# Two graph layers on one core: where the loads of x, of the turned x1 and of the transposed codes are issued

## The chip, the cores and the metric

The kernel runs on one core of a Trainium2 chip. Its engines are TensorE (PE, with its weight loads listed apart as PEld), VectorE (DVE), ScalarE (ACT), GpSimd (POOL) and SyncE (SP). SP, ACT and POOL also issue DMA transfers, each from its own instruction stream and in that stream's order. The metric is device time in microseconds, the median of several runs of the whole kernel; lower is better.

## The reference

Two layers work on x (4096 x 512, float32) with one 0/1 matrix adj (4096 x 4096, about 0.8% ones). In the code below, cut to what matters, `ln` is a normalisation of each row.

```python
# layer 0: mean over the first 64 neighbours
Ab   = adj > 0
keep = Ab & (cumsum(Ab, axis=1) <= 64)
cnt  = keep.sum(axis=1, keepdims=True)
xj   = leaky_relu((keep @ x) / maximum(cnt, 1) @ W_nb.T + b_nb)
xi   = leaky_relu(x @ W_line.T + b_line)
x1   = ln(x + xi + where(cnt > 0, xj, 0))

# layer 1: attention over the neighbours
Wh  = x1 @ W + bW
e   = leaky(Wh @ a1 + b1)[:, None] + (Wh @ a2 + b2)[None, :]   # slope 0.2 on the sum
att = softmax(where(adj > 0, e, -9e15), axis=1)
out = ln(x1 + att @ Wh)
```

## The kernel before

The 4096 rows are cut into 32 blocks of 128. The order of the instructions on each engine is the order in which the program writes them, and waits on data and on buffers are added to it. A pool of n buffers makes the n+1st tile wait until the first is no longer read or written. There are four stages.

**Maps of layer 0 (loop over i at L332 to L375, 0 to 272 us).** For each block i, PE turns x (`turn_x`, four 128x128 transposes into `pt`, copied to `xt` by ACT), one block ahead, and multiplies the turned block by the two weight matrices (`linear`, L288, eight matmul instructions each). ACT copies the first product to `y_hi`, DVE keeps the remainder in `y_lo` (L373). DVE's `own(i)` (L319 to L321) adds bias, activation and x to the second product and stores it to `own_d`; its last operation (L321) is the last reader of the tile `xb` of x, which has four buffers. So `load_x(i + 2)` (L238, a DMA issued by ACT for i of 3 and above) needs `own(i - 2)` to be done. From block 5 on the loop also makes codes of adj (`codes_until`): SP loads a piece of 2048 columns (`a`, 1 MB), ACT makes `edge` of it, DVE scans it (`left`, L169, and the product at L174), ACT packs the result to bytes (`code`, L192) and POOL stores it to `code_d`. 22 of the 64 pieces are made in this stage. Before the codes, in block 2, DVE folds the layer-1 weights (`fold_w`) and SP stores the 4 KB result in 4-byte elements (`wa_d`) and loads it back spread over the partitions (`wa_row`).

**Sums of layer 0 (272 to 736 us).** PE adds up, for each block, 64 products of 0/1 maps (`kt`, made by ACT from transposed codes) with `y_hi` and `y_lo` (L433). The remaining codes are made beside it, and finished blocks go through the normalisation and are stored to `x1_d`.

**Maps of layer 1 (loop over i at L656, 736 to 869 us).** For each block, `wh` = x1 times W (L661, eight matmul instructions). x1 comes back from `x1_d` already arranged (`load_turned(i + 3)`, L469: four DMAs of 64 KB issued by ACT), DVE finishes the turn in 32x32 squares (`turn_x1(i + 2)`, L491), PE multiplies. The tile `x1b` has four buffers, so the load of block b needs block b-4 to have been turned by DVE. Blocks 0 and 1 are loaded by SP in another form and turned on PE. In the same loop SP loads untransposed codes (`nat`, one buffer, `load_nat`, L510), and in blocks 12 to 19 ACT and DVE take maxima over them (`greatest`, L523 and L527); at block 6 SP issues the four transposing loads of codes for the first group of four blocks (`load_ct(0)`, L506). At block 22 `shifts(0)` (L544, L546) has SP store eight small numbers per row (`uv_d`) and load them back spread over the partitions (`row`), once the store has landed.

**Sums of layer 1 (869 to 1765 us).** In eight groups of four blocks, ACT and DVE make the attention weights (`produce`) and PE multiplies them with `wh` (L601). In each group SP loads the transposed codes of the next one (`load_ct(g + 1)`, two buffers), nat, uv_d and row again.

The built program gives every DMA issued by SP or ACT one of eight completion semaphores in turn, so such a DMA also waits for the one that used its semaphore before, eight DMAs earlier in the program.

Of the kernel before, what the change touches and what calls it, by code (L numbers as in the profile page):

```python
# [11 lines left out]
BF16 = mybir.dt.bfloat16  # L12
# [8 lines left out]
P = 128  # L21
# [10 lines left out]
def two_layer_adj_gnn(  # L32
# [16 lines left out]
    nc = tc.nc  # L49
# [3 lines left out]
    NT = NB // 2  # L53
    CH = 2048
    NCH = N // CH
    GB = 4
# [53 lines left out]
    code_d = [dram.tile([P, N // 2], BF16, name=f"code_d{b}") for b in range(NB)]  # L110

    def transpose_to(dst, src_of, n):

        pt = ps_s.tile([P, n, P], F32, name="pt")
        for k in range(n):
            nc.tensor.transpose(pt[:, k, :], src_of(k), ident)  # L116
        nc.scalar.copy(dst, pt)  # L117
# [20 lines left out]
    with ExitStack() as l0:  # L138
# [88 lines left out]
        with ExitStack() as la:  # L227
# [7 lines left out]
            def load_x(i):  # L235
                if i < NB:
                    xbs[i] = work.tile([P, C], F32, name="xb", bufs=4)
                    (nc.sync if i < 3 else nc.scalar).dma_start(xbs[i], x_blk(i))  # L238

            def turn_x(i):  # L240
                if i < NB:
                    xts[i] = work.tile([P, NC, P], F32, name="xt")
                    transpose_to(xts[i], lambda k: xbs[i][:, ts(k, P)], NC)
# [30 lines left out]
            def turn_w(name, idle=0):  # L274

                wt = wp.tile([P, NC, C], F32, name=f"wt_{name}")
                for c in range(NC):
                    if idle:
                        spin(idle)
                    transpose_to(  # L280
                        wt[:, :, ts(c, P)], lambda k: raw[name][c][:, ts(k, P)], NC
                    )
                w_t[name] = wt

            def linear(lhs_t, name):
                pl = ps_acc.tile([P, C], F32, name="acc")
                for k in range(NC):
                    nc.tensor.matmul(  # L288
                        pl, lhs_t[:, k, :], w_t[name][:, k, :],
                        start=(k == 0), stop=(k == NC - 1),  # L290
                    )
                return pl
# [24 lines left out]
            def own(i):  # L317
                t = work.tile([P, C], F32, name="t")
                nc.vector.tensor_tensor(t, pls.pop(i), bias_line, ALU.add)  # L319
                nc.vector.scalar_tensor_tensor(t, t, 0.01, t, ALU.mult, ALU.max)  # L320
                nc.vector.tensor_tensor(t, t, xbs.pop(i), ALU.add)  # L321
                nc.gpsimd.dma_start(own_d[i], t)
# [9 lines left out]
            for i in range(NB):  # L332
                if i == 0:
                    nc.sync.dma_start(bias_line, b_line.partition_broadcast(P))
                if i > 0:
                    turn_x(i + 1)
                xt = xts.pop(i)
                pys[i] = linear(xt, "nb")
                if i == 0:
                    turn_w("line")  # L340
                pls[i] = linear(xt, "line")
                if i == 0:
                    turn_x(1)
                nc.scalar.copy(y_hi[:, i, :], pys[i])
                if i > 0:
                    own(i - 1)
                if i > 0:
                    load_x(i + 2)
                if i == 0:
                    load_w("w", w, (nc.sync,))  # L350
                if i == 1:
                    load_rows()
                    nc.gpsimd.dma_start(bias_nb, b_nb.partition_broadcast(P))
                if i == 2:
                    fold_w()
                if i == 3:
                    spread_wa()
                if i > 3:
                    codes_until(int((i - 3) * 22 / (NB - 6)) if i < NB - 3 else 22)
                if i == NB - 3:  # L360

                    spare = adj_p.tile([P, CH], I32, name="a")
                    ktbs[0] = spare[:, : CH // 2].bitcast(BF16).rearrange(
                        "p (t i) -> p t i", t=NT
                    )
                    nc.sync.dma_start_transpose(ktbs[0], code_d[0])
                if i == NB - 1:
                    spare = adj_p.tile([P, CH], BF16, name="edge")
                    kts[0] = spare.bitcast(F32R).rearrange(
                        "p (t r i) -> p t r i", r=2, i=P  # L370
                    )
                    make_kt(0)
                nc.vector.tensor_tensor(  # L373
                    y_lo[:, i, :], pys.pop(i), y_hi[:, i, :].bitcast(F32), ALU.subtract
                )  # L375
# [44 lines left out]
        for s in range(NB * NS):  # L420
            i, g = divmod(s, NS)
# [27 lines left out]
    ctp = tile_p("l1_ct", 2)  # L449
# [16 lines left out]
    x1rs, x1bs, x1ts, pws, cts, nats, uvs, ms = {}, {}, {}, {}, {}, {}, {}, {}  # L466
    p_ts, accs1, zs, zaccs, ys = {}, {}, {}, {}, {}

    def load_turned(i):  # L469

        if i < NB:
            x1rs[i] = xp.tile([P, P // SQ, NC, SQ], F32, name="x1b", bufs=4)
            for n in range(NC):
                nc.scalar.dma_start(
                    x1rs[i][ts(n, SQ)].rearrange("a j m b -> a j (m b)"),
                    x1_d[i][:, ts(n, P)].rearrange("(j a) c -> a j c", a=SQ),
                )
# [21 lines left out]
        else:  # L499
            nc.vector.tensor_tensor(wh_sum, wh_sum, wh[:, i, :], ALU.add)  # L500

    def load_ct(g):
        if g < NG:
            cts[g] = ctp.tile([P, NT, GB, P], BF16, name="ct")
            for k in range(GB):
                nc.sync.dma_start_transpose(cts[g][:, :, k, :], code_d[g * GB + k])  # L506

    def load_nat(b):
        nats[b] = xp.tile([P, N // 2], BF16, name="nat", bufs=1)
# [146 lines left out]
    for i in range(NB):  # L656
        load_turned(i + 3)
        pw = ps_acc.tile([P, C], F32, name="acc")
        x1t = x1ts.pop(i)
        for k in range(NC):  # L660
            nc.tensor.matmul(  # L661
                pw, x1t[:, k, :], ws[:, k, :], start=(k == 0), stop=(k == NC - 1)
            )
        pws[i] = pw
        turn_x1(i + 2)
        if i == 4:
            load_nat(0)
        if i == 6:
            load_ct(0)
        if 12 <= i < 12 + 2 * GB:  # L670
            greatest(*divmod(i - 12, 2))
        if i == 22:
            shifts(0)
        if i > 0:
            finish_wh(i - 1)
        if i >= NB - LEAD:
            produce(i - NB + LEAD)
# [3 lines left out]
    for q in range(LEAD, NQ + LEAD):  # L681
        g, t = divmod(q, NT)
        if q < NQ:
            produce(q)
        consume(q - LEAD)
        if q == 8:
            all_sum = ps_acc.tile([P, C], F32, name="acc")
            nc.tensor.matmul(all_sum, ones, wh_sum, start=True, stop=True)
            nc.scalar.copy(wh_sum, all_sum)
        if t == LEAD and g < NG:  # L690
            load_ct(g + 1)
            if g + 1 < NG:
                load_nat((g + 1) * GB)
        if q == NQ - 2:
            for k in range(GB):
                load_x1(NB - GB + k)
        if q == NQ + LEAD - 1:

            end_weights(NG - 1)
            for k in range(GB):  # L700
                b, base = NB - GB + k, x1bs.pop(NB - GB + k)
                share = stat.tile([P, 1], F32, name="share")
                nc.vector.tensor_tensor(
                    share, none[:, b : b + 1], zs[NG - 1][:, k : k + 1], ALU.mult
                )
                nc.vector.scalar_tensor_tensor(base, wh_sum, share, base, ALU.mult, ALU.add)
                x1bs[b] = base
            for k in range(GB):
                b = NB - GB + k
                y = ep.tile([P, C], F32, name="y", bufs=4)  # L710
                nc.vector.scalar_tensor_tensor(
                    y, accs1[NG - 1][k], zs[NG - 1][:, k : k + 1], x1bs.pop(b),
                    ALU.mult, ALU.add,
                )
                ys[b] = y, ln_stats(y)
                end_out(b, nc.sync)
            break

        if t == LEAD - 1 and g > 0:
            for k in range(GB):  # L720
                load_x1((g - 1) * GB + k)
                end_sum((g - 1) * GB + k)
            end_weights(g - 1)
        if g > 0:
            if LEAD <= t < LEAD + GB:
                end_stats((g - 1) * GB + t - LEAD)
            if LEAD < t <= LEAD + GB:
                end_out((g - 1) * GB + t - LEAD - 1, nc.gpsimd)
        if g + 1 < NG:
            if 5 <= t < 5 + 2 * GB:  # L730
                k, h = divmod(t - 5, 2)
                greatest((g + 1) * GB + k, h)
            if t == 13:
                shifts(g + 1)
# [34 lines left out]
```

## Time and profile before

| | |
|---|---|
| runs | 1764.3, 1766.97, 1770.71 us (median 1766.97) |
| profiled execution | 1767.0 us, of which the span of the trace 1764.9 us |
| PE busy | 1720.0 us (97%) |
| DVE, ACT, POOL busy | 1402.2, 875.3, 192.9 us |
| chain that ended last | PE 84%, DVE 8%, DMA 5% |
| x loads by ACT (29) | 256 KB each, median 3.2 us from issue to landing |
| turned x1 by ACT (120 DMAs) | 64 KB each, median 2.1 us to landing |
| transposing loads of codes (32) | median 5.6 us to landing |

Busy time is the sum over an engine's instructions; the span is from the first to the last of them. The chain that ended last is followed back from the end: at each step to what released the instruction, or to the one before it on its engine. The idle time of an engine matters only where that chain passes through it. A PE that is called busy in the first stage can still be waiting between short matmul groups, so that stage is read from the chain and the timelines, not from the shares.

### The profile page before, as it was taken

How to read it: one execution, taken by the hardware profiler on the slowest of the kernel's cores; microseconds unless marked ns; L12 is line 12 of the kernel's file. 1: busy time of each engine (PE TensorE's matmuls, PEld its weight loads, DVE VectorE, ACT ScalarE, POOL GpSimd, SP SyncE). 2: the span in 40 equal slices, each digit the busy share in tenths (PEclk: the TensorE clock that was granted, in tenths of full speed). 3: DMA queues.
4: the chain of work that ended last, by engine and by line, in shares of the span. 5: the costliest groups of instructions: out<-in, count | busy, mean ns of one | idle time of the engine just before them, and what ended most of it. 6: DMA issues, size and time to landing. Idle time of an engine off the chain costs nothing.

```text
span 1764.9 us, 14748 instructions
## 1 busy us (share of the span) xinstructions
PE 1720.0 (97%) x5118; PEld 949.6 (54%) x5118; DVE 1402.2 (79%) x1649; ACT 875.3 (50%) x910; POOL 192.9 (11%) x234
## 2 busy tenths in 40 slices
PE   8799999999999999989899999999999999999998
PEld 5344447888888888733344444444444444444443
DVE  3599998999999997458677986968869689696754
ACT  2355555767667674112355463644636445364331
POOL 1011112223232322100000100001000010000100
PEclk9899999999999999999999999999999999999999
DMA  4566667676767673762402304122041220411100
GB/s 143 191 220 204 205 222 204 192 221 198 221 203 210 207 204 95 133 148 79 100 25 55 88 24 96 60 64 68 24 95 56 65 68 27 96 50 46 48 0 25
DMA packets 209227, 206.57 MB, mean 117 GB/s; under 512 B 154848, under 2 KB 170240, under 8 KB 200832
## 3 DMA queue, kind: packets, MB, share of 16 engines
q1 hardware_dynamic: 174352, 145.55, 30.8%
q0 software_dynamic: 13056, 44.07, 6.6%
q10 hardware_dynamic: 21744, 16.00, 3.4%
q8 instruction: 41, 0.67, 0.2%
q14 instruction: 34, 0.28, 0.1%
HBM read 130.02 MB, written 42.00 MB: 97 GB/s over the span
## 4 chain that ended last, share of the span: by engine, by line
PE 84%; DVE 8%; DMA 5%; issue 1%; SPq 1%; ACT 1%; ACTq 0%; POOLq 0%; DVEq 0%
PE acc L601 49%; PE acc L433 26%; PE acc L288 5%; DVE left L169 3%; PE acc L661 2%; DMA xb<-in_x_dram 2%; DMA ct<-code_d 1%; SPq L506 1%; PE pt L116 1%; DMA x1b<-x_d 1%; DVE pen L527 1%; DVE t L320 1%; DVE y_lo L373 1%; DMA uv_d<-uv 1%; DVE t L319 1%
## 5 line engine op out<-in xcount | busy, mean ns | idle before, releaser
L601 PE MATMUL acc<-wh,p 128*128 128x512 f32 x2048 | 881.2, 592 | 0.0
L601 PEld LDWEIGHTS acc<-wh,p 128*128 128x128 f32 x2048 | 388.5, 190 | 486.0 <-issue 485.3
L433 PE MATMUL acc<-y_lo,kt 128*128 128x512 f32 x1016 | 395.2, 389 | 0.0
L433 PE MATMUL acc<-y_hi,kt 128*128 128x512 f32 x1016 | 395.2, 389 | 0.0
L561 ACT ACTIVATE p<-row,e 128x512 f32<-128x512 f32 x256 | 182.8, 714 | 419.1 <-PE acc L601 367.4
L564 DVE TENSOR_TENSOR p<-p,p 128x1024 f32<-128x1024 f32 x128 | 156.2, 1221 | 124.7 <-ACT p L561 124.6
L127 POOL TENSOR_TENSOR rs<-ve,neg_half 128x1 f32<-128x1 f32 x64 | 101.5, 1587 | 1152.1 <-DVE ve L125 1152.1
L221 ACT ACTIVATE kt<-ktb,steep 128x1024 fp32r<-128x1024 uint8 x124 | 142.8, 1152 | 154.2 <-PE acc L433 154.2
L433 PEld LDWEIGHTS acc<-y_hi,kt 128*128 128x128 f32 x1016 | 190.8, 188 | 39.5
L433 PEld LDWEIGHTS acc<-y_lo,kt 128*128 128x128 f32 x1016 | 190.8, 188 | 39.5
L561 ACT ACTIVATE p<-row,e_fifth 128x512 f32<-128x512 f32 x256 | 180.8, 706 | 1.4 <-DVE p L564 1.3
L566 DVE TENSOR_TENSOR p<-p,ct 128x1024 f32<-128x1024 f32 x128 | 156.8, 1225 | 4.4
L523 ACT ACTIVATE pen<-nat,far 128x2048 bf16<-128x2048 uint8 x64 | 127.3, 1990 | 63.4 <-DMA x1b<-x_d 52.1
L571 DVE TENSOR_TENSOR zacc<-zacc,p 128x1024 f32<-128x1024 f32 x120 | 147.0, 1225 | 4.1
L169 DVE TENSOR_TENSOR_SCAN left<-two,edge 128x2048 bf16<-128x2048 f32 x32 | 141.4, 4417 | 6.4 <-ACT edge L158 6.4
L169 DVE TENSOR_TENSOR_SCAN left<-two,ends,edge 128x2048 bf16<-128x2048 f32 x32 | 143.3, 4478 | 0.0
L158 ACT ACTIVATE edge<-a,steep 128x2048 bf16<-128x2048 int32 x64 | 127.5, 1993 | 17.8 <-DVE left L174 10.5
L661 PE MATMUL acc<-ws,x_t 128*128 128x512 f32 x256 | 116.0, 611 | 16.0 <-DVE x_t L491 15.8
L192 ACT CAST code<-left 128x2048 uint8<-128x2048 bf16 x64 | 120.5, 1883 | 0.8 <-DVE left L174 0.8
L288 PE MATMUL acc<-wt_nb,xt 128*128 128x512 f32 x256 | 119.2, 610 | 0.9 <-ACT wt_nb L117 0.7
L288 PE MATMUL acc<-wt_line,xt 128*128 128x512 f32 x256 | 115.2, 592 | 0.7 <-ACT wt_line L117 0.7
L661 PEld LDWEIGHTS acc<-ws,x_t 128*128 128x128 f32 x256 | 49.1, 195 | 82.4 <-issue 57.0
(103 smaller groups left out, 1029.1 us busy)
## 6 DMA issues: line engine op xcount, KB each, us to landing
a<-in_adj_dram SPq DMA_DIRECT2D x64, 1024.0 KB, 5.5
code_d<-code POOLq DMA_DIRECT2D x64, 256.0 KB, 4.4
nat<-code_d SPq DMA_DIRECT2D x32, 512.0 KB, 3.6
own_d<-t POOLq DMA_DIRECT2D x32, 256.0 KB, 4.3
own<-own_d SPq DMA_DIRECT2D x32, 256.0 KB, 2.8
x_d<-own POOLq DMA_DIRECT2D x32, 256.0 KB, 3.4
x1b<-x_d SPq DMA_DIRECT2D x32, 256.0 KB, 5.5
x1b<-x_d ACTq DMA_DIRECT2D x120, 64.0 KB, 2.1
```

The source lines that it names most:

```text
L158: nc.scalar.activation(edge_of[s], loaded.pop(s), AF.Sigmoid, bias=steep[:, 0:1], scale=STEEP)
L169: nc.vector.tensor_tensor_scan(left, two.to_broadcast([P, CH]), e, NEIGHBORS + 2.0 if h == 0 else end, ALU.max, ALU.subtract,)
L221: nc.scalar.activation(kts[s], bytes_.rearrange("p t (i r) -> p t r i", r=2), AF.Sigmoid, bias=steep[:, 1:2], scale=STEEP,)
L288: nc.tensor.matmul(pl, lhs_t[:, k, :], w_t[name][:, k, :], start=(k == 0), stop=(k == NC - 1),)
L433: nc.tensor.matmul(accs[i], kt[:, k // 2, k % 2, :], term[:, j, :], start=(j == 0 and term is y_hi), stop=(j == NB - 1 and term is y_lo),)
L523: nc.scalar.activation(pen, nats[b].bitcast(U8)[:, ts(h, HALF)], AF.Relu, bias=far, scale=-FAR)
L561: nc.scalar.activation(dst[:, r, :], uvs[g][:, k, :], AF.Exp, bias=e[:, b : b + 1])
L564: nc.vector.tensor_tensor(p0, p0, p1, ALU.max)
L566: nc.vector.tensor_tensor(p0, p0, code.rearrange("p (x r) -> p r x", r=2), ALU.min)
L571: nc.vector.tensor_tensor(zaccs[g], zaccs[g], p0, ALU.add)
L601: nc.tensor.matmul(accs1[g][k], p_[:, r, ts(k, P)], wh[:, 2 * t_ + r, :], start=(t_ == 0 and r == 0), stop=(t_ == NT - 1 and r == 1),)
L661: nc.tensor.matmul(pw, x1t[:, k, :], ws[:, k, :], start=(k == 0), stop=(k == NC - 1))
```

## The change

Three things move; no computation is added or taken away. In the maps of layer 0, `load_x(i + 2)` is issued at the top of block i, ahead of `turn_x(i + 1)`, instead of behind `own(i - 1)`; on ACT's stream it now stands before the copies of `xt` and `y_hi` of that block. In the maps of layer 1, the four DMAs of each turned x1 block are issued by SP instead of ACT, in SP's stream order with nat, uv_d, row and the transposing loads. And the four transposing loads of the first group, issued together at block 6 before, are issued one by one at blocks 8, 11, 14 and 17, each behind the x1 loads of its block; the later groups keep their four loads together.

```diff
                 if i > 0:
+                    load_x(i + 2)
                     turn_x(i + 1)
...
                 if i > 0:
                     own(i - 1)
-                if i > 0:
-                    load_x(i + 2)
...
             for n in range(NC):
-                nc.scalar.dma_start(
+                nc.sync.dma_start(
                     x1rs[i][ts(n, SQ)].rearrange("a j m b -> a j (m b)"),
...
-    def load_ct(g):
+    def load_ct(g, k):
         if g < NG:
-            cts[g] = ctp.tile([P, NT, GB, P], BF16, name="ct")
-            for k in range(GB):
-                nc.sync.dma_start_transpose(cts[g][:, :, k, :], code_d[g * GB + k])
+            if k == 0:
+                cts[g] = ctp.tile([P, NT, GB, P], BF16, name="ct")
+            nc.sync.dma_start_transpose(cts[g][:, :, k, :], code_d[g * GB + k])
...
-        if i == 6:
-            load_ct(0)
+        if i in range(8, 8 + 3 * GB, 3):
+            load_ct(0, (i - 8) // 3)
...
         if t == LEAD and g < NG:
-            load_ct(g + 1)
+            for k in range(GB):
+                load_ct(g + 1, k)
```

## The prediction

> **What bounds the kernel now.** I read the page first, then the stages, the chain of waits, and the timelines of the two stages that the change touches.
>
> Stages (start:end, sum; then PE, PEld, DVE, ACT, POOL busy, granted clock, DMA share, GB/s):
>
> ```profile
> 0.00:69.80 69.80, 58.27 (x181) 31.16 (x182) 20.85 (x48) 16.54 (x25) 6.84 (x17) 0.95 0.46 151
> 69.80:271.60 201.80, 193.01 (x513) 87.49 (x511) 197.81 (x196) 109.63 (x95) 25.17 (x47) 0.99 0.63 208
> 271.60:736.20 464.60, 464.60 (x2051) 384.60 (x2050) 407.13 (x526) 297.19 (x211) 115.54 (x107) 1.00 0.66 193
> 736.20:869.00 132.80, 116.79 (x266) 49.94 (x265) 85.18 (x129) 24.83 (x22) 2.90 (x4) 0.96 0.58 127
> ```
>
> From 271.6 to 736.2 PE never stops, and from 869.0 on it stops for 8.7 us only. Neither stage holds an edited line that can cost it anything. What can be won or lost lies before 271.6 (maps of layer 0) and in 736 to 869 (maps of layer 1); whatever moves their ends moves the kernel's end by as much, since PE-bound work follows.
>
> The chain of waits in the first stage, in order of time (start, duration):
>
> ```profile
> 33.17 3.91 DMA xb<-in_x_dram
> ...
> 41.38 9.64 DMA xb<-in_x_dram
> ...
> 57.90 3.71 DMA xb<-in_x_dram
> ...
> 67.75 2.01 ACT edge L158
> 69.78 4.44 DVE left L169
> ...
> 253.41 4.12 DMA xb<-in_x_dram
> 257.66 0.63 PE pt L116 x4
> 258.29 13.73 PE acc L288 x32
> 272.02 464.23 PE acc L433 x2048
> ```
>
> Up to 69.8 PE waits for x. From there DVE is the limit: 197.8 of 201.8 us busy, and its only wait of note there (6.4 us) is the one that ends as its first scan starts at 69.78. So x that lands earlier helps after 69.8 only through the start of that first scan and at the very end.
>
> The last stage, PE, DVE and SP timelines (start, duration; in brackets idle before and what ended it):
>
> ```profile
> 755.17 8.83 PE L661 MATMUL acc<-ws,x_t 128*128 128x512 f32 x16 [3.81 <-DVE x_t L491]
> 765.40 41.47 PE L661 MATMUL acc<-ws,x_t 128*128 128x512 f32 x96 [1.40 <-DVE x_t L491]
> ```
> ```profile
> 834.43 0.71 DVE L491 STREAM_TRANSPOSE x_t<-x1b 128x512 f32<-128x512 f32 x1 [1.42 <-PE acc L661]
> 847.27 0.71 DVE L491 STREAM_TRANSPOSE x_t<-x1b 128x512 f32<-128x512 f32 x1 [10.83 <-DMA x1b<-x_d]
> ```
> ```profile
> 736.28 14.10 SPq L506 DMA_TRANSPOSE ct<-code_d  x4
> 829.01 0.38 SPq L544 DMA_DIRECT2D uv_d<-uv  x1
> 838.30 0.33 SPq L546 DMA_DIRECT2D row<-uv_d  x1
> 838.68 14.50 SPq L506 DMA_TRANSPOSE ct<-code_d  x4
> ```
>
> A block is eight L661 matmuls, 41.47/12 = 3.45 us. Twice x1 comes late, each time while four transposing loads run: at 748 to 765 and at 838 to 863.
>
> **Edit 1, x at the top of the block.** One 0.33 us DMA issue per block is moved ahead of the copies of xt and y_hi on ACT; nothing is added. It still needs its buffer back from block i-2, that is the last DVE operation of own (L321). If that is late, the xt copy, y_hi, edge and code of the block wait behind it on ACT, and DVE's scan waits for edge.
>
> Early blocks. PE needs 0.44+3.44+3.44 = 7.3 us a block. Block 3's transposes could run at 36.35 and later ones at 43.7 and 51.0. x of block 5 is now asked for after y_hi of block 2 (33.7) instead of 41.38; its buffer is free at 31.3. So the 9.64 us load leaves the path. Block 6's load waits for own of block 2 (L321, 41.03+0.69) and goes at 41.8, into the same 4-byte write wa_d (37.44, 11.8 us) that the slow load met. I give it 9.64 too: 51.4, so PE waits 0.5. nb of block 5 ends at 55.4 and y_hi starts at 55.5, against 65.85 before. In the built kernel the table load that follows also stands behind the first piece of adj: issued at 49.73, and the three of that window took 8.8 us in the median, so 58.5. Then table load 1.28 (59.8), edge 2.0 (61.8), first scan at 61.85 against 69.78: **7.9 us**. Bounds: 6 with adj at 60.4 (its longest, 10.6), 9.5 with 7.2. What is late next is adj, not x.
>
> Steady part. DVE takes 8.4 us per block with a scan and PE 7.3, so the short PE waits for x (1.4, 1.0, 1.2 us and smaller) bring nothing. ACT reaches the load after its code copy, which itself waits for the scan's product; y_lo and own are done 2.7 us after that product, edge and code take 3.8, so ACT is held by at most 1 us and PE does not wait for it. Cost zero; its cover is that xt is copied a block ahead (if that were gone, 1 us in each of 22 blocks).
>
> End. The last x load went at 253.41 behind y_hi; now behind the code copy, ending at 251.72: **1.7 us** (0 to 2.5). First stage: 9.6.
>
> **Edits 2 and 3, x1 by SP, code loads spread.** 120 issues move from ACT to SP: four a block, median 0.44 us, about 1.96 with the gaps, below 3.45. SP's stage then holds also three nat loads, the transposes (14.1/4 = 3.5 us of issuing each) and uv_d with row. ACT is freed; it was idle, so that pays nothing by itself.
>
> Start. x1 of blocks 4 to 6 no longer meets transposes, which come behind x1 of block 11 on. PE, starting at 737.37, would begin block 6 at 737.37+6x3.45 = 758.1 instead of 765.40: **7.3 us**. Each moved transpose holds SP 3.5 us and lands by 5.6 (median). A block's load may go when the buffer of four blocks before comes free, 13.8 us before it is due, so three blocks' issues and one transpose (9.4 us) fit into 10.3. Cost zero.
>
> Maps with maxima (790 to 823) stay at DVE's 4.14 us a block. nat waits for the ACT copy of the half before it (15.6 us in three waits already) and x1 now stands behind nat; the block concerned is due three blocks later, 12.4 us. Zero.
>
> New wait. uv_d and row used to be passed by x1 on ACT's queue. Now x1 of blocks 26 to 31 stands behind row, and row behind uv_d's landing. With the 7.3 us: uv ready 821.6, uv_d lands 9.3 later (830.9), row goes, x1 of block 26 is issued 831.2 to 833.0. No row shows x1 behind row in one queue. Lower bound 835.1 (2.1, an x1 DMA's median), upper 841 (row's 6.6, then 3 more as in the 2.7 median). I take 837.5: row's median 5.8 from 830.9, then 0.8 for the 256 KB. DVE's transpose and PE then start block 26 at 838.3, after some 8 us of idling (due 830.2). Six blocks of 3.45 and 2.0 for the slow clock after such a stop (8.91 for sixteen matmuls at 848.03 against 6.9) give 861.0, against 869.0: **8.0 us** in all for the stage, 4.5 to 10.5. The old stall, 9 to 13 us by the same uv_d and the second group of transposes, is thus replaced by an earlier one of like size; those transposes now come behind the last x1.
>
> The Trainium skill, page "DMA: Bandwidth & Descriptors", section "Queues, rings and completion order", speaks against this edit: SP and ACT own a ring each on every DMA engine, the engine takes its rings in turn, and within one ring descriptors are consumed in order. By that x1 gives up its own turn and stands fully behind row. By it the 837.5 would hold, and without it 835.1, which makes the stage 10.4. The trace bears it out only in part: the x load at 41.38 had ACT's ring to itself and still took 9.64 us beside wa_d on SP's.
>
> **Sum.** 7.9+1.7+8.0 = 17.6; 1764.9-17.6 = 1747.3 us of span. The profiled run's time was 1767.0, 2.1 more than its span, and the median shown is 1766.97: so 1749 us.
>
> **Rivals.**
> (a) The load at the top is hidden anyway: buffers come back too late, or adj sets the first scan where it was. For it: DVE's 98% and the wait for own; against it: PE's idle 0.7, 6.5 and 0.5 us and its slow restart before 69.8, some 10 us in all. Then only the 8.0 remain: 1759.
> (b) The change in layer 1 does not do what it says: the stall behind row takes back the start (x1 of block 26 at 845 or later, as two of the longest landings in a row). For it: the long serial uv_d, row, x1. Then the first stage alone: 1757.
> (c) Nothing to measure: (a) and (b) together, 1767.
> (d) Slower. x1 in one queue with transposes arrives late at each of the four. Longest issue 6.1 and longest landing after it 11.9 (the chain's load at 745.08), behind 1.9 of x1's own issuing and 2.1 of landing: 22.0 us after the buffer came free, where 3.45+13.8 = 17.2 is allowed. That is 4.8 late, with 2.0 for the clock 6.8, times four 27: 1749+27 = 1776. It decides from 5.8 us each ((17.6+5.3)/4) on. Against it: those long numbers came with four transposes back to back; singly the medians are 2.8 and 5.6. The ring order of the page named above would be the mechanism.
>
> **Chances.** Forecast 62%, (a) 10%, (b) 13%, (c) 7%, (d) 8%. About 0.3% (5.3 us) can be told from no change. Forecast, (a) and (b) are faster by more: 85%; within: 7%; slower: 8%. The forecast's own bounds are first stage 6 to 12, last 4.5 to 10.5 and one or two us of spread: 1743 to 1758. The range takes in (a) and (b) with some spread, and the case that both bounds are beaten: 1740 to 1761.
>
> **What would show it.** First scan near 62 and PE without a stop over 1 us for xb before 69; L433 starting near 262. In layer 1 PE unbroken to about 806, the only long DVE wait for x1 the one that row ends, at some 828 (837.5 less the 9.6 of the first stage), L601 starting near 851 instead of 869. Wrong would be: a scan that starts later than 66, waits of DVE for ACT edge, a PE stop of over 3 us at a block after a transpose, or a stop longer than 12 us behind row.

## The result, and the profile after

| | before | after |
|---|---|---|
| time, median of 6 runs | 1765.78 us (1764.3 to 1770.71) | 1750.65 us (1749.81 to 1751.98) |
| span of the profiled execution | 1764.9 us | 1748.2 us |
| first scan on DVE | 69.78 | 60.59 |
| first L433 / L432 (the changed file is one line shorter from here on) | 271.46 | 261.52 |
| sums of layer 0, from there to the next stage | 464.6 long | 464.66 long |
| last stage, from its first turn on PE to the first L601 / L600 | 132.9 long | 126.06 long |

The ratio is 0.991, with a 95% interval of 0.9898 to 0.9921. Of the 16.7 us that the span lost, 9.9 lie in the first stage (271.46 - 261.52) and 6.8 in the last (132.9 - 126.06); the stage between them and everything behind 852 are as they were. Over the profiles of this study the sums of layer 0 take 464.6 to 464.7 us (but for experiment 4, which edits them), and the part behind the last stage 895.9 to 896.1. The last stage varies more where it is left as before: it is 132.9 us in the profile of before, and 136.9 and 136.15 in those of experiments 1 and 3, so by these three the 6.8 is at the low end of what the change brings there.

The stages of the changed kernel, with the columns of the prediction's first view (start:end, length; busy PE, PEld, DVE, ACT, POOL; granted clock, DMA share, GB/s):

```profile
0.00:60.59 60.59, 56.64 (x188) 29.69 (x189) 20.83 (x48) 16.52 (x25) 6.83 (x17) 1.00 0.54 174
60.59:261.52 200.93, 188.83 (x505) 86.59 (x504) 196.95 (x195) 109.16 (x95) 24.86 (x46) 0.99 0.62 209
261.52:726.18 464.66, 464.66 (x2051) 384.51 (x2050) 407.78 (x527) 297.21 (x211) 115.72 (x107) 1.00 0.66 192
726.18:852.24 126.06, 114.70 (x265) 49.82 (x264) 85.78 (x130) 25.93 (x24) 2.90 (x4) 0.96 0.58 136
```

From the first scan on DVE is busy for 196.95 of 200.93 us, as before (197.81 of 201.80): the same work begins 9.2 us earlier and so ends earlier. In the chain of waits the x loads ahead of the first scan are gone, and adj stands in their place (start, duration):

```profile
35.81 12.35 DMA wa_d<-wa
...
48.61 8.56 DMA a<-in_adj_dram
...
57.26 1.28 ACT L158
...
58.55 2.01 ACT edge L158
...
60.59 4.44 DVE left L169
```

The first piece of adj waits on SP for wa_d to land (SP issues `wa_row` behind it, and adj behind that), then takes 8.56 us; table load and edge follow at once. The last stage, PE's timeline and then SP's:

```profile
727.45 62.07 PE L660 MATMUL acc<-ws,x_t 128*128 128x512 f32 x144 [0.24 <-ACT x_t L117]
...
806.47 14.00 PE L660 MATMUL acc<-ws,x_t 128*128 128x512 f32 x32 [0.49 <-DVE x_t L490]
829.44 22.96 PE L660 MATMUL acc<-ws,x_t 128*128 128x512 f32 x48 [8.98 <-DVE x_t L490]
```

```profile
754.82 2.45 SPq L505 DMA_TRANSPOSE ct<-code_d  x1
...
763.27 2.40 SPq L505 DMA_TRANSPOSE ct<-code_d  x1
...
811.65 0.38 SPq L543 DMA_DIRECT2D uv_d<-uv  x1
820.74 0.34 SPq L545 DMA_DIRECT2D row<-uv_d  x1
821.14 14.40 SPq L473 DMA_DIRECT2D x1b<-x_d  x24
835.59 11.33 SPq L505 DMA_TRANSPOSE ct<-code_d  x4
```

PE now runs 144 matmuls, 18 blocks, without a stop, past the four single transposes; the two stops of 3.81 and 1.40 us at the start of the stage are gone. One stop is left, 8.98 us: between uv_d at 811.65 and row at 820.74 SP issues nothing, and the 24 remaining loads of x1 (blocks 26 to 31) all stand behind row. That stop costs more than its length: the 48 matmuls behind it take 22.96 us, where six blocks at 3.45 us (62.07/18) take 20.7.

### The profile page after: what moved, and what is told of

The parts are those of the page before. It is cut to its first block, busy times and chain, and to the rows that moved or that the text cites. A ratio compares the mean times of both kernels' runs of the same rounds, so it can differ in the third digit from the quotient of the medians.

```text
span 1748.2 us, 14749 instructions
## 1 busy us (share of the span) xinstructions
PE 1712.2 (98%) x5118; PEld 947.0 (54%) x5118; DVE 1402.0 (80%) x1649; ACT 874.6 (50%) x910; POOL 192.7 (11%) x234
## 4 chain that ended last, share of the span: by engine, by line
PE 83%; DVE 11%; DMA 3%; issue 2%; ACT 1%; SPq 0%; POOL 0%; ACTq 0%; POOLq 0%; DVEq 0%
PE acc L600 50%; PE acc L432 27%; DVE left L169 5%; PE acc L660 4%; PE acc L288 1%; DVE t L320 1%; DVE y_lo L372 1%; DVE t L319 1%; DVE t L321 1%; DVE pen L526 1%; DMA wa_d<-wa 1%; DMA xb<-in_x_dram 1%; DMA uv_d<-uv 1%; DMA a<-in_adj_dram 0%; DVE left L174 0%
## 5 line engine op out<-in xcount | busy, mean ns | idle before, releaser
L600 PE MATMUL acc<-wh,p 128*128 128x512 f32 x2048 | 881.2, 592 | 0.0
L600 PEld LDWEIGHTS acc<-wh,p 128*128 128x128 f32 x2048 | 388.5, 190 | 486.0 <-issue 485.5
L432 PE MATMUL acc<-y_lo,kt 128*128 128x512 f32 x1016 | 395.2, 389 | 0.0
L432 PE MATMUL acc<-y_hi,kt 128*128 128x512 f32 x1016 | 395.2, 389 | 0.0
L432 PEld LDWEIGHTS acc<-y_hi,kt 128*128 128x128 f32 x1016 | 190.8, 188 | 39.7
L432 PEld LDWEIGHTS acc<-y_lo,kt 128*128 128x128 f32 x1016 | 190.6, 188 | 39.5
```

Of the source, the lines that this page charges most:

```text
L432: nc.tensor.matmul(accs[i], kt[:, k // 2, k % 2, :], term[:, j, :], start=(j == 0 and term is y_hi), stop=(j == NB - 1 and term is y_lo),)
L600: nc.tensor.matmul(accs1[g][k], p_[:, r, ts(k, P)], wh[:, 2 * t_ + r, :], start=(t_ == 0 and r == 0), stop=(t_ == NT - 1 and r == 1),)
```

## The experiments

Every experiment was timed in five rounds against the kernel before on the same chip. Where the base is not the kernel before, it is the changed one.

**1. Edit 1 alone.** The kernel before with x loaded at the top of the block, and nothing else; that is the changed kernel without edits 2 and 3.

```diff
                 if i > 0:
+                    load_x(i + 2)
                     turn_x(i + 1)
...
                 if i > 0:
                     own(i - 1)
-                if i > 0:
-                    load_x(i + 2)
```

> Only edit 1 (x asked for at the top of the block); layer 1 as before. Theory (the two halves add up; edit 1 works through the first scan): first scan near 61, first sum matmul (L432) near 262, layer 1's maps still some 132.7 us with PE stops of 3.8 and 6.8 us; time before less 8 to 10, about 1757. Rival (the gain is all in layer 1, x is hidden by DVE): equal to before, 1766.

Measured: 1759.93 us against 1768.52, ratio 0.996 (0.9945 to 0.9976); that is 8.6 us by the medians and 7.1 by the ratio. First scan at 61.21, L432 at 262.05. In the last stage PE stops for 3.66, 4.94, 6.81 and 2.03 us, at about the places where it did before the change (3.81, 1.40, 6.78 and 1.64), and the stage took 136.9 us in this execution where 132.7 were expected. So the first part of the sum stands on its own.

**2. Edits 2 and 3 alone.** The changed kernel with x loaded behind `own` again.

```diff
                 if i > 0:
-                    load_x(i + 2)
                     turn_x(i + 1)
...
                 if i > 0:
                     own(i - 1)
+                if i > 0:
+                    load_x(i + 2)
```

> Only edits 2 and 3 (turned x1 by SP, code loads spread); x as before. Theory: layer 0 as before (first scan near 69.8), layer 1's maps some 6.7 us shorter than 132.7 with one PE stop of about 9 us behind row; about 1759. Rival (the stall behind row takes it all back unless the first stage is faster): 1766.

Measured: 1758.67 us, ratio 0.9951 (0.9936 to 0.9965). First scan at 68.23; the chain there runs through an x load again (56.15, 3.91 us). In the last stage 144 matmuls unbroken from 735.59, and one stop of 8.55 us behind row. The two parts add up: 1 - 0.996 and 1 - 0.9951 give 0.0089, and the whole change 1 - 0.991 = 0.0090.

**3. Is it the early blocks that pay?** The kernel before, with x at the top of the block in blocks 1 to 5 alone.

```diff
+                if 0 < i < 6:
+                    load_x(i + 2)
                 if i > 0:
                     turn_x(i + 1)
...
-                if i > 0:
+                if i > 5:
                     load_x(i + 2)
```

> The kernel before with x asked for at the top in blocks 1 to 5 only; from block 6 on where it was. Theory (x helps only through the first scan; in the steady part DVE covers it): all of edit 1 but its last 0.5 to 1.7 us, so 6 to 9 us below before, as edit 1 alone. Rival (the many short waits for x over 26 blocks are what edit 1 removes): at most 2 to 3 us below before.

Measured: 1758.77 us against 1766.69, ratio 0.9956 (0.9941 to 0.997), first scan at 61.10. Five of the 29 moved loads bring what all of them bring (0.996): what edit 1 is worth, it is worth through the first scan.

**4. Is DVE really what sets the end of the first stage?** The changed kernel with two scans fewer there, 20 instead of 22; the next stage makes them, at a faster pace.

```diff
-                    codes_until(int((i - 3) * 22 / (NB - 6)) if i < NB - 3 else 22)
+                    codes_until(int((i - 3) * 20 / (NB - 6)) if i < NB - 3 else 20)
...
-        RATE = 1.5
+        RATE = 1.6
```

> The changed kernel with 20 instead of 22 pieces of codes made in the maps of layer 0; the other two are made in the next stage (rate 1.6 a block instead of 1.5). Theory (DVE sets the length of the first stage after its first scan): two scans with their product, 5.8 us each, leave the stage, until PE's own 7.3 us a block takes over: L432 starts 8 to 11.6 us earlier, and the next stage does not get longer; about 1740. Rival (PE and its x loads set the end): within 2 us of the changed kernel.

Measured: 1753.65 us, ratio 0.9927 (0.9914 to 0.9941). The first stage ends at 252.06, 9.5 us earlier: DVE did set it. But the sums of layer 0 take 477.1 us instead of 464.7, and all of it and more is given back. That the next stage would stay as long was wrong. The chain of waits shows what happens there, again and again:

```profile
420.56 1.88 ACT code L192
422.44 1.06 ACT kt L221
423.50 0.04 issue
423.55 14.86 PE acc L432 x64
```

A `code` on ACT stands ahead of the `kt` that PE needs next. Of the 12.4 us PE idles 8.45 (477.11 long, 468.66 busy). The 22 scans of the first stage are thus what the stage behind it can't take without PE waiting.

**5. Which of edits 2 and 3 pays: x1 on SP?** The changed kernel with x1 issued by ACT, the transposes still spread. It was run twice, the second time on one chip with the changed kernel.

```diff
-                nc.sync.dma_start(
+                nc.scalar.dma_start(
                     x1rs[i][ts(n, SQ)].rearrange("a j m b -> a j (m b)"),
```

> The changed kernel with the turned x1 issued by ACT again, the code loads still spread over blocks 8, 11, 14, 17. Theory: nothing on SP's stream holds the first two transposes back any more, so they go at the start of the stage and meet x1 of blocks 4 to 6; and the second group's four transposes meet x1 of the last blocks again. Some 3 to 6 us slower than the changed kernel: about 1755. Rival (spreading in the program text is what counts): within 1.5 us of the changed kernel's 1750.7.

> The changed kernel with the turned x1 issued by ACT as before, the transposes still spread, once more beside the changed kernel. Theory: x1 on SP is worth 1 to 3 us, by the trace of the first such run 0.9 (its stop behind the second group's transposes, 6.8 us, in place of the one behind row, 9.0, and one more of 1.8 at the first transposes): 1751 to 1755 us, and above the changed kernel in the same rounds. Rival: it is worth nothing that can be told, the medians stand within 1 us of each other.

> The changed kernel once more, beside the next run on the same chip. Both theories: 1750 to 1753 us.

Measured: 1754.76 us, ratio 0.9931 (0.9916 to 0.9946), and 1751.92 us (1748.49 to 1756.71), 0.9927 (0.9911 to 0.9944), beside the changed kernel with 1749.32 us (1747.34 to 1749.59), 0.9907 (0.9894 to 0.9921). The intervals of that last pair overlap a little, so the 2.6 us between the medians are likely but not settled. The two profiled executions differ from each other by more: in the first the last stage is 0.9 us longer than the changed kernel's, in the second 7.2 (PE stops of 1.18, 3.37 and 6.40 us). With x1 on SP the time also varies less: 2.2 and 2.3 us lie between the fastest and the slowest execution of a run, against 5.6 and 8.2 with x1 on ACT. Both runs still stop for over 6 us near uv_d (6.76 and 6.40), and the chain of the first says why:

```profile
814.13 9.32 DMA uv_d<-uv
823.47 0.36 ACTq L473
...
824.35 7.91 DMA x1b<-x_d
...
832.38 0.72 DVE x_t L490
833.15 9.97 PE acc L660 x16
```

ACT issues its next x1 load 0.02 us after uv_d, SP's transfer, has landed (814.13 + 9.32 = 823.45). Nothing in ACT's own stream asks for that. The built program does: of the x1 block in hand, the load that has to go next waits for the completion semaphore that uv_d uses (number 105 for both in this trace), one of the eight which SP and ACT share. The kernel before did the same, in ACT's timeline:

```profile
825.72 0.32 ACTq L474 DMA_DIRECT2D x1b<-x_d  x1
...
838.26 0.84 ACTq L474 DMA_DIRECT2D x1b<-x_d  x2
```

Its uv_d went at 829.01 and landed at 838.23. Of x1 of block 27 the first load is issued at 825.72 and the second, which waits for uv_d's semaphore and for nothing else, at 838.26. So x1 did not pass uv_d on ACT's queue. (Two more profiles with x1 on ACT, experiment 1 and the second run here, show the same: 832.16 and 827.41, each within 0.05 us of uv_d's landing.)

**6. Which of edits 2 and 3 pays: the spreading?** The changed kernel with all four transposes at block 6, x1 still on SP.

```diff
-        if i in range(8, 8 + 3 * GB, 3):
-            load_ct(0, (i - 8) // 3)
+        if i == 6:
+            for k in range(GB):
+                load_ct(0, k)
```

> The changed kernel with all four transposing loads at block 6 on SP, x1 on SP. Theory: the four hold SP for 10 to 14 us behind x1 of block 9, which is about the whole lead of four blocks, so x1 of block 10 is 3 to 9 us late: PE stop there, 1754 to 1760. Rival (being behind x1 on SP suffices, spreading is needless): 1750 to 1752.

Measured: 1754.87 us, ratio 0.9931 (0.9915 to 0.9947). SP is held by the four transposes for 14.55 us, and the block behind them is late on DVE, by SP's and DVE's timelines:

```profile
745.43 14.55 SPq L505 DMA_TRANSPOSE ct<-code_d  x4
```

```profile
763.95 0.71 DVE L490 STREAM_TRANSPOSE x_t<-x1b 128x512 f32<-128x512 f32 x1 [7.25 <-DMA x1b<-x_d]
```

PE stops for 3.21 us there and runs slowly after it; the last stage takes 130.9 us instead of 126.1. Here the wait is in the open: in one stream, x1 stands behind the transposes. With one transpose every third block it is covered.

**7. The stop that is left.** The changed kernel with uv_d and row of the first group issued by POOL, which has a stream and completion semaphores of its own.

```diff
-        nc.sync.dma_start(uv_d[g].rearrange("k b p -> p k b"), uv)
+        queue = nc.gpsimd if g == 0 else nc.sync
+        queue.dma_start(uv_d[g].rearrange("k b p -> p k b"), uv)
...
-        nc.sync.dma_start(
+        queue.dma_start(
```

> The changed kernel with uv_d and row of the first group issued by POOL, not SP. Theory (the stop of 9 us and its slow restart of 2.3 come from x1 standing behind row on SP's stream): the stop is gone, L600 starts 10 to 11 us earlier, about 1740. Rival A (data path: x1 is slow because row's data and the small elements of uv_d occupy the DMA engines): the stop stays above 5 us, over 1746. Rival B (POOL's transfers land so late that the first weights wait): a new stop before L600.

Measured: 1738.28 us (1737.78 to 1740.37), ratio 0.9843 (0.9827 to 0.9859), its interval clear of the changed kernel's. POOL's timeline and PE's (this file is one line longer, so L661 and L601):

```profile
811.60 0.90 POOL L544 DMA_DIRECT2D uv_d<-uv  x1 [68.45 <-DVE uv L542]
822.63 0.56 POOL L546 DMA_DIRECT2D row<-uv_d  x1 [10.13 <-DMA uv_d<-uv]
```

```profile
806.16 34.60 PE L661 MATMUL acc<-ws,x_t 128*128 128x512 f32 x80 [0.49 <-DVE x_t L490]
840.59 4.88 PE L601 MATMUL acc<-wh,p 128*128 128x512 f32 x11
```

uv_d takes 10.7 us instead of 9.1 and row goes 1.9 us later than in the changed kernel, but x1 no longer waits for either: ten blocks run in 34.60 us, and the sums start at 840.59 instead of 852.24. The stage began 0.3 us earlier (727.14), so the stop cost 852.24 - 840.59 - 0.3 = 11.3 us: 9.0 of idling and 2.3 of slow clock. So it was x1's place behind row in SP's stream that made the stop. The transfers are in each other's way all the same: the eight x1 loads that SP issues from 814.07 to 818.80, while uv_d is in flight, take 8.0 to 10.2 us, against a median of 2.0 before it. They cost nothing, because they are loads of blocks 29 and 30, asked for early enough: block 29 has landed at 825.3 and is due at some 830. Whether POOL would do as much with x1 left on ACT wasn't tried.

**8. Is adj late because of wa_d? First try.** The changed kernel with the load `wa_row` (the call of `spread_wa`) moved to block 8, so that adj is asked for behind wa_d's issue and not behind its landing.

```diff
-                if i == 3:
+                if i == 8:
                     spread_wa()
```

> The changed kernel with the load of wa_row moved from block 3 to block 8, so that the first pieces of adj are no longer behind the landing of wa_d on SP's stream. Theory (after the change adj, not x, sets the first scan): adj issued near 36 instead of 48.6, the ACT table load right after y_hi of block 5, first scan 3 to 4 us earlier, about 1747. Rival (PE and x still set it): first scan within 1 us of 60.6.

Measured: 1755.5 us, ratio 0.9939 (0.9925 to 0.9953), a miss: adj is asked for at 36.27, and the first scan starts at 65.38, later than the changed kernel's 60.59. The chain of waits:

```profile
40.10 15.40 DMA xb<-in_x_dram
55.49 0.14 issue
55.63 1.09 PE pt L116 x4
```

The x load that was issued while wa_d and adj were both in flight takes 15.40 us, against 9.17 in the changed kernel, and PE stops for it (6.42 us). The two pieces of adj take 15.0 and 18.3 us themselves. SP's wait for wa_d had kept adj and this load out of each other's way.

**9. Second try, from two starts.** On top of experiment 7, wa_d and wa_row are both issued at block 8, so that adj waits for nothing and no 4-byte store is in flight while the early x loads run, and the codes begin at block 4, or at block 3.

```diff
                 nc.vector.tensor_tensor(ca, ca, b12, ALU.add)
+            def spread_wa():
                 nc.sync.dma_start(wa_d.rearrange("k (c p) -> p k c", p=P), wa)
-            def spread_wa():
                 nc.sync.dma_start(
...
-                if i == 3:
+                if i == 8:
...
-                    codes_until(int((i - 3) * 22 / (NB - 6)) if i < NB - 3 else 22)
+                    codes_until(min(22, int((i - 2) * 22 / (NB - 6))))
```

From block 3 it is `(i - 1)`, with one block more in the condition ahead of it. The store of wa_d thus belongs to `spread_wa` now, ahead of the load of `wa_row`.

> The run with uv_d and row of the first group issued by POOL, and in addition wa_d and wa_row both issued by SP at block 8 instead of block 2 (so that SP never waits for the landing of wa_d ahead of the first piece of adj), and the codes of the first stage begun at block 4 instead of block 5, 22 scans as before. Theory: the start of the first scan sets the end of the first stage, because DVE does not stop behind it; the first piece of adj then waits for nothing, and with wa_d out of the way the x loads take 3 to 4 us. First scan at 50 to 54 (60.6 in the changed kernel), first linear of the second stage at 253 to 256 (261.5; PE's own limit was near 252 in the run with two scans fewer), time 1738 - 6 = 1732 us (1729 to 1734). Rival, from the run with wa_row at block 8: the 1 MB pieces of adj, asked for early, make x late whatever wa_d does (an x load of 15 us at block 6), and the first scan stays at 60 or later: 1738 to 1742.

> As the run with the codes begun at block 4, but begun at block 3. Theory: first scan at 43 to 47, but the first stage can end no earlier than PE's own work allows, near 252: so at most 1 to 3 us below the run from block 4, 1728 to 1732 us. Rival: two pieces of adj among the first x loads make x late and PE stops for it by over 5 us: no faster than the run from block 4, or slower.

Measured: 1738.43 us, 0.985 (0.9836 to 0.9863), and 1738.19 us (1735.95 to 1738.62), 0.9844 (0.983 to 0.9858): nothing beyond experiment 7's 0.9843, and a miss both times. The first scan comes as expected, at 50.54, or a little sooner, at 42.34, and the first L432 stands at 262.90 and 260.92 all the same (261.23 in experiment 7). SP's timeline and the chain of the run from block 4:

```profile
67.44 0.39 SPq L311 DMA_DIRECT2D wa_d<-wa  x1
80.76 0.33 SPq L312 DMA_DIRECT2D wa_row<-wa_d  x1
```

```profile
50.54 4.44 DVE left L169
...
67.59 12.41 DMA xb<-in_x_dram
...
80.14 1.09 PE pt L116 x4
81.22 8.87 PE acc L288 x16
...
263.46 464.23 PE acc L432 x2048
```

The slow x load has moved with the store. wa_d is in flight from 67.4 to 80.8, the x load issued at 67.59 takes 12.41 us where the median of that window's x loads is 3.1, PE stops for 7.21 us, and eight matmuls after it take 5.64 us instead of 3.60. DVE, whose scans are handed out by the blocks that PE has done, loses the start that it had. Neither theory had this. A piece of adj was in flight as well (issued at 67.02), but it is not enough by itself: the x load issued as close behind a piece of adj at 59.09, with no wa_d, took 6.20 us. The early scan alone was not enough.

## Why the prediction was right, and where it was not

**First stage: right, 9.9 for 9.6, and so close by some luck.** The first scan was put at 61.85 and came at 60.59. "What is late next is adj, not x" holds by the chain, and the 9.64 us load left it: x of block 6 met wa_d as said, landed 2 us before the 51.4 given, and PE waited 0.17 us for it instead of 0.5. Of the 1.26 us between forecast and scan, 1.1 are adj, asked for at 48.61 instead of 49.73 because wa_d landed sooner. Some of the 9.2 us may be the execution's and not the change's: the two profiles in which x is loaded as before have their first scan at 69.78 and 68.23, and the nine in which x goes early and adj's order is kept have it at 60.0 to 61.2. So the gain lies between 7.0 and 9.8, with the 7.9 inside. The end of the stage was over-sized: 9.94 - 9.19 = 0.75 us instead of 1.7, because the last x load, issued 2.0 us earlier than before when counted from the first scan (181.67 after it instead of 183.63), took 5.33 us and not 4.12. The scan brought 1.3 us more than was put and the end 1.0 less, and in the sum the two nearly cancel.

**Steady part: right at zero, with a wait that was not seen.** A PE stop of 4.04 us for x appears at 75.6, larger than any that the prediction named behind 69. It costs nothing, since DVE is the limit there; experiment 3 shows the same from the other side.

**Start of the last stage: right.** PE is unbroken for 18 blocks, and no block behind a transpose is late. That takes away rival (d), whose mechanism is real but needs the transposes together: experiment 6 shows it. (The longest landing of a transpose in the profile of before is 12.3 us, for the one issued at 741.39, and not the 11.9 of rival (d); it changes little there.)

**The stop behind row: right in place and kind, mis-sized by 1.2.** x1 of block 26 was to land 6.6 us after row was issued (830.9 to 837.5). It landed at 828.50, 7.8 after row's 820.74. That is the 1.2 us by which the stage's 8.0 became 6.8; the six blocks behind it, with their slow clock, took 22.8 us to the first L600 for the 22.7 given. By the rule cited from the Trainium skill, page "DMA: Bandwidth & Descriptors", section "Queues, rings and completion order", x1 on SP's ring stands behind row and x1 on ACT's would have its own turn. The runs show no such turn: in the first run of experiment 5, with x1 on ACT, x1 landed 8.8 us after row was issued (823.51 to 832.3). There four transposes followed row at once, so the rule is not disproved. Where row went by POOL (experiments 7 and 9), the first two x1 loads that SP issued behind it landed 4.9 to 6.7 us after row was issued, against 6.3 to 7.3 with both on SP. That is the most that speaks for a lower price here, and the transfers around them are not the same.

**One step was wrong, without harm to the sum: "uv_d and row used to be passed by x1 on ACT's queue".** They were not. Experiment 5 and ACT's timeline of the kernel before show x1 on ACT held until uv_d lands, by the shared semaphores, a rule that the description of the kernel states and the prediction did not apply. So the new wait was no new cost: the old stop hung on the same transfer, and the move of x1 to SP put one wait, in the stream's order, in the place of another. It fits this that x1 on ACT differs so little in experiment 5. It did no harm because the 8.0 was reckoned from the new stop alone; the old one does not enter it. The start of the old stage shows the same: by the chain of before, ACT issues x1 at 756.96, 0.01 us after a transpose has landed (745.08 + 11.87 = 756.95), and x1 and the codes have no data in common; the semaphores are the only link between the two (103 for both in the trace).

Rivals (a), (b) and (c) fall with experiments 1 and 2, each of which shows its part alone and clear of no change.

## What to carry to other kernels

A transfer that must land before the next instruction of its stream holds everything behind it, and with completion semaphores given out in turn it also holds other queues that share them: put the slow round trip (store, wait, load) on a queue that shares neither, as experiment 7 did for 11.3 us, before reordering the loads around it. A load that starts an engine which then never stops is worth its whole lead, but only while the pace of the work behind it does not depend on something else that is late; an early scan brought nothing once PE was stopped for x later on. And a slow neighbour is not got rid of by moving it; look at what it will meet in its new place.

## What the runs showed of the hardware that was not expected

A 4 KB store in 4-byte elements is slow for others, not only for itself. wa_d took 11.3 to 13.9 us over all fourteen profiles. The first 256 KB x load issued while it was in flight took 8.0 to 12.4 us, or 15.4 with adj beside it, against medians of 3.1 to 6.9 us in the same stretches; one issued in its last 5 us took 4.0 to 5.5 us (10.4 with adj). When the store was moved by 31 us, the slow load moved with it. What is ahead of the store isn't held: the piece of adj issued 0.42 us before it in experiment 9 took 6.1 us, about as the pieces around it. uv_d, the other 4 KB store in 4-byte elements, does the same: in experiments 7 and 9 the 64 KB x1 loads issued behind it took 7.0 to 10.2 us, against a median of 2.0. That it is the stores' elements that do it was not tried by itself.

A stop of PE can cost more than its length, and the length alone doesn't say whether. The granted clock falls to half for one to three whole pieces of 3.41 us (10.24 us around the end of the 8.98 us stop, from 823.45 to 833.69), and the matmuls in them run slower. Over the fourteen profiles, from 28 us on, no PE stop of under 2.1 us came with such a piece. Of the 17 stops from 2.10 to 3.92 us 13 did and four did not (2.15, 3.66, 3.88 and 3.92 us), and all longer ones did. Behind a stop that came with one the matmuls lost 1.2 to 3.2 us against the full pace. The shortest such stop is in experiment 2, 2.10 us long and ended at 156.23 (the columns are those of the stages):

```profile
153.12:156.53 3.41, 1.31 (x6) 0.51 (x5) 3.31 (x6) 1.74 (x1) 0.00 (x0) 1.00 0.57 225
156.53:159.95 3.42, 3.42 (x7) 1.65 (x6) 3.39 (x3) 2.54 (x3) 1.08 (x2) 0.50 0.64 163
```

The Trainium skill, page "TensorE: Matmul & The Clock Gate", section "Part 1: The HAM clock gate (the "warmup" mystery)", has the clock go down after an idle window of some 3.4 us that runs freely and does not begin with the stop. The length of the pieces agrees with it, and so do stops of like length that fare differently. That such a window has to be idle throughout the trace does not bear out: PE was busy for 1.31 of the 3.41 us ahead of the fall shown here.
